# Attention inside a fused attention and feed-forward kernel: a projection in two steps over two turns, and weighted sums counted in half blocks of 256 queries

## The chip, the cores and the metric

The kernel runs on one core of a Trainium2 chip. The metric is the device time of one launch in microseconds (us). Its engines are TensorE (PE in the profile, matmuls; PEld are its weight loads), VectorE (DVE), ScalarE (ACT), GpSimd (POOL) and SyncE (SP, here a queue that issues DMAs). Each engine takes its instructions in the order of the program, and waits at each until what it needs has been made.

## The reference, cut to what matters

The input is 4 batches of 1024 tokens with 256 features.

```python
x = x + layernorm(attention(layernorm(x)))     # 16 heads of 16 features, softmax over 1024 keys
x = x + layernorm(ffn(layernorm(x)))           # silu gate, two 1024x1024 layers with gelu, 1024 -> 256

qkv    = xn @ Wqkv.T
scores = q @ k.T / 4                           # per batch and head, 1024 x 1024
attn   = exp(scores - max) / (sum + 1e-6)
y      = (attn @ v) @ Wout.T
```

The change lies in the attention alone. The kernel computes exponentials without subtracting the maximum first, folds the greatest exponential in later (the `top` tiles), and falls back to a general version if a bound says that this isn't safe.

## The kernel before, in words

**Tiles and units.** The attention is a list of 512 tiles (L514): for each of 4 batches b, 4 groups g of 4 heads, 2 halves h of 512 queries, 8 blocks c of 128 keys, and 2 pairs u of heads. Sixteen tiles make a unit (b, g, h). For one tile, `exponentials` (L520) issues two score matmuls into one of three PSUM buffers (`s`, two banks each) and one ScalarE instruction that writes `e` into a ring in SBUF that holds 8 tiles (`RING`). For two tiles of the same c, which I call a block, `weigh` (L530) multiplies the exponentials of 4 heads with the values of the block's keys: 4 matmuls over 512 queries, each of which the profile shows as two instructions (float32), so 8 instructions for a block. They add up in `acc`, one PSUM bank, over the 8 blocks of a unit. `rise` (L537) keeps the greatest exponential of each query on VectorE. At the end of a unit `unit_end` (L760) transposes `acc` out on VectorE, and `divide` adds the steps that normalise.

**Turns.** The loop at L1335 runs in turns. A turn makes 3 tiles (`TURN`, L1339; `make` keeps at most 8 tiles made and not yet weighed), then weighs blocks made in earlier turns, one or two of them: all that are there, but only one where `side.next_is_heavy()` says that a heavy step comes next (L1346). With 3 tiles to a turn, turns with one block and with two alternate. A unit's end cuts the weighing of its turn short (L1357), since `acc` has one buffer. Then the turn calls `side.take` (L1366).

**Side work.** All other attention work is cut into `Step`s (L74), which stand in chains in `Side` (L663). In each turn `take` (L697) runs at most one step that uses TensorE, and as many others as `room` allows, which is a budget of VectorE time: `ROOM` less what `rise` took, less the work of the tensor step that comes. `gap` is the least number of turns after the step before in its chain. A step built with `heavy=True` is also `patient` (L79), unless set otherwise (L754, L771): it isn't run in a turn that is `tired`, that is, one that weighed two blocks, or the one after a heavy step (L681, L712, L1362).

**The steps that the change touches.** `project` of the prologue (L378) makes q or k of one half of the queries for 8 heads of the next batch: 8 matmuls (two over the features, c, times four slots), 16 instructions in the profile as `p` at L321, into the one PSUM bank of the pool `misc` (L258). Then ScalarE copies the rounded high part (`cq..hi`, `ck..hi`, L386) and VectorE computes the low part (`lo`, L387); both read the bank. There are 8 such steps for each batch; of those for the first batch 4 run ahead of the loop. `values` (L368) makes v: 32 instructions, `pv`. `project` of `ending` (L613) is the output projection: 32 instructions, `py`. All three take their bank from `misc`, and so do the transposes (`pt`, 4 instructions), the bounds (`pn`, 2) and the flag (`pr`, 6).

**What hangs on the projections.** When all of a group's q and k are there, `stack` (L489) copies them into the operands of the scores (`sk`, `sq`) with 32 DMAs on the SP queue, 4 or 6 in a turn. `begin` (L728) builds the next batch's chain, in which the second half of the heads (`qk1`) comes with a gap of 2 turns.

After the last tile the feed-forward part runs, which the change leaves as it is.

Of the kernel before, what the change touches and what calls it, by code (L numbers as in the profile page):

```python
# [22 lines left out]
SLOT = 32  # L23
# [4 lines left out]
RING = 8  # L28
TURN = 3
# [44 lines left out]
class Step:  # L74


    def __init__(self, run, gap=0, tensor=True, heavy=False, work=0):
        self.run, self.gap, self.tensor, self.heavy, self.work = run, gap, tensor, heavy, work
        self.ready, self.patient = lambda: True, heavy  # L79


class Norms:
# [47 lines left out]
def tile_fast(ctx: ExitStack, tc: tile.TileContext, x, wqk, wv, wo, w1, w1s, w2, w2s, h1, h1s, h2, h2s, w3, w3s, out, bad):  # L130
# [65 lines left out]
    with ExitStack() as actx, ExitStack() as rctx:  # L196
# [132 lines left out]
        def prologue(b, space, copy):  # L329
# [36 lines left out]
                return run  # L366

            def values(t0):  # L368
                def run():
                    pv = space(f"pv_{b}_{t0}").rearrange("p (t d) -> p t d", d=D)  # L370
                    for i in range(2):
                        for c in range(DC):
                            by_slots(pv[:, i, :], st["xT"][:, c, (t0 + i) * P : (t0 + i + 1) * P], wv_sb[:, c, :], start=c == 0, stop=c == DC - 1)
                    copy(cv[:, t0 : t0 + 2, :], pv)

                return run

            def project(w, m, h):  # L378
                def run():
                    pp = space(f"p{w}_{b}_{m}_{h}")  # L380
                    for c in range(DC):
                        heads = wqk_sb[:, c, w, HPT * m : HPT * (m + 1), :].rearrange("p h d -> p (h d)")
                        by_slots(pp, heads, st["xT"][:, c, h * NQ : (h + 1) * NQ], start=c == 0, stop=c == DC - 1)
                    hi, lo = (cq[w, m, k][:, h * NQ : (h + 1) * NQ] for k in ("hi", "lo"))
                    scale = 1.0 if w else 1.0 / math.sqrt(DH)
                    to_scalar(hi, pp, scale)  # L386
                    nc.vector.scalar_tensor_tensor(lo, pp, scale, hi.bitcast(F32), ALU.mult, ALU.subtract)  # L387

                return run
# [63 lines left out]

            norm = [[Step(gather(h, i), 1, False, work=1.6) for i in range(0, TPQ, 2)] + [Step(root(h), 0, False, work=0.3)] for h in range(NH)]
            xt = [[Step(apply(h, i), 1, False, work=1.2) for i in range(0, TPQ, 2)] + [Step(transposes(h, c), 1 if c else 2, work=1) for c in range(DC)] for h in range(NH)]
            qk = [[[Step(project(w, m, h), 1, heavy=True, work=1) for w in (1, 0)] for h in range(NH)] for m in range(DC)]
            v = [Step(values(t), 1, heavy=b > 0, work=1) for t in range(0, NT, 2)]
            flags = []
            for m in range(DC):
                flags.append([Step(total(m), 1, False, work=1.7)])  # L460
# [66 lines left out]
                nc.tensor.matmul(s[:, a, :], stacks[1, g % 2, u][r, c * P : (c + 1) * P], stacks[0, g % 2, u][r, h * NQ : (h + 1) * NQ], start=True, stop=True)  # L527
            nc.scalar.activation(pair(k)[:, u], s, AF.Exp)  # L528

        def weigh(k, acc):  # L530

            b, g, _, c, _ = tiles[k]
            assert slotted[g % 2][:2] == (b, g) and c < slotted[g % 2][2]
            for i in range(HPG):
                nc.tensor.matmul(acc[SLOT * i : SLOT * (i + 1), :], vaug[g % 2][:, c, i, :], pair(k)[:, i // 2, i % 2, :], start=c == 0, stop=c == NT - 1)  # L535

        def rise(k):  # L537

# [61 lines left out]
        def ending(b, h, copy):  # L600

            st = {}

            def transposes(c):
                def run():
                    if c == 0:
                        st["oT"] = work.tile([P, DC, NQ], F32, tag="oT", name=f"oT_{b}_{h}", bufs=1)
                        st["y"] = (both if h else work).tile([P, TPQ, D], F32, tag="y", name=f"y_{b}_{h}", bufs=1)
                    nc.vector.transpose(st["oT"][:, c, :], on[h][:, c].rearrange("p j s -> p (j s)"))

                return run

            def project(t0):  # L613
                def run():
                    py = misc(f"py_{b}_{h}_{t0}").rearrange("p (t d) -> p t d", d=D)
                    for i in range(2):
                        for c in range(DC):
                            by_slots(py[:, i, :], st["oT"][:, c, (t0 + i) * P : (t0 + i + 1) * P], wo_sb[:, c, :], start=c == 0, stop=c == DC - 1)
                    (copy if b == B - 1 else to_scalar)(st["y"][:, t0 : t0 + 2, :], py)
# [31 lines left out]
            steps = [Step(transposes(c), 1, False, work=0.7) for c in range(DC)] + [Step(project(t), 2, heavy=True) for t in range(0, TPQ, 2)]  # L651
            tail = (
                [Step(gather(i), 1, False, work=1.6) for i in range(0, TPQ, 2)] + [Step(root, 0, False, work=0.3)]
                + [Step(apply(i), 2 if b == B - 1 and not i else 1, False, work=1.2) for i in range(0, TPQ, 2)] + [Step(residual(i), 1, False, work=1) for i in range(0, TPQ, 2)]
            )
            if b < B - 1:

                return steps + [Step(lambda: side.add(tail), 0, False)]
            opened = Step(open_ffn, 0, False)
            opened.ready = lambda: not ends[b, 0][0]  # L660
            return steps + ([opened] if h == NH - 1 else []) + tail

        class Side:  # L663


            def __init__(self):
                self.first, self.rest, self.slot = [], [], 0
                self.room = 0.0
                self.tired = False

            def add(self, steps, first=False):
                chain = [list(steps), self.slot]
# [24 lines left out]
            def take(self, room=math.inf, spare=0.0):  # L697
# [30 lines left out]
        def begin(b):  # L728

            if b + 1 < B:  # L730
# [29 lines left out]
        def unit_end(b, g, h):  # L760
# [544 lines left out]
        for h in range(NH):  # L1305
            for step in xt[h][TPQ // 2 :]:
                step.run()
            for w, step in zip((1, 0), qk[0][h]):
                if (h, w) == (0, 0):
                    compact(0)  # L1310
                step.run()
# [14 lines left out]
        made = seen = weighed = 0  # L1326

        def make(end):

# [5 lines left out]
        while weighed < len(tiles):  # L1335
            n = end = made
            end += TURN
            before, risen = weighed, seen
            make(end)  # L1339
            if made == len(tiles):  # L1340
                n = made
# [1 line left out]
                rise(k)  # L1343
                seen += 2

            if n - weighed >= 4 and made - weighed + TURN - 2 <= RING and tiles[weighed][3] != NT - 2 and side.next_is_heavy():  # L1346
                n = weighed + 2
            while weighed + 2 <= n:
                b, g, h, c, _ = tiles[weighed]
                if c == 0:  # L1350
                    accs[b, g, h] = ps_acc.tile([P, NQ], F32, tag="acc", name="acc")
                weigh(weighed, accs[b, g, h])
                weighed += 2
                if c == NT - 1:
                    unit_end(b, g, h)
# [254 lines left out]
```

## Time and profile before

| | before |
|---|---|
| median of 3 runs | 1233.38 us (1233.04 to 1235.36) |
| the profiled execution's own time | 1230.5 us |
| its span | 1228.7 us |
| mean granted TensorE clock | 0.991 |
| 30 to 190 us: busy PE, DVE, ACT | 151.15, 107.83, 134.06 us of 160 |
| 190 to 331 us | 136.01, 103.48, 124.30 us of 141 |
| 331 to 472 us | 137.77, 102.92, 125.91 us of 141 |
| 472 to 594 us | 111.14, 85.78, 112.72 us of 122 |

The loop over the turns runs from about 30 to 594 us of the span; the four stretches are roughly the four batches. What follows to 1228.7 us is the feed-forward part. A row of the profile gives the line, the engine, the operation, what is written and read, the shapes, and how many instructions there were; a row of the timeline gives start and length in us of instructions of the same kind that follow on each other. Matmuls overlap, so that a group's length is longer by its last instruction's tail than the time until the next group starts; where I give the cost of a group on PE, I take the distance from its start to the next group's start.

### The profile page before, as it was taken

What the parts mean: (1) busy time and instruction counts of PE and PEld (TensorE: products, weight loads), DVE (VectorE), ACT (ScalarE), POOL (GpSimd) and SP (SyncE); (2) the same over time, 40 slices, a digit from 0 to 9 for tenths busy, and PEclk for the clock granted to TensorE, in tenths of its full rate; (3) what the DMA queues carried; (4) which work ended last, traced back from release to release, by engine and by line L of the source; (5) the groups of instructions that cost most, each with busy time, mean ns of one, the idle gap of its engine ahead of it and who ended that gap; (6) DMA issues with size and microseconds to landing.
All of it is one profiled execution on the core that took longest, in us unless ns stands there. A gap on an engine that the chain in (4) does not pass through costs nothing.

```text
span 1228.7 us, 20496 instructions
## 1 busy us (share of the span) xinstructions
PE 1168.3 (95%) x7618; PEld 697.0 (57%) x7618; DVE 841.3 (68%) x1500; ACT 884.7 (72%) x1049; POOL 204.4 (17%) x279
## 2 busy tenths in 40 slices
PE   7999999999999999989999999999999999999993
PEld 2333333333333333323578888877888878888783
DVE  3577579865787667667685756867578676784756
ACT  4788798998889899998557565576656766566651
POOL 6212124444435342000000000000000000000000
PEclk9999999999999999999999999999999999999997
DMA  5675756766566676554314341354512545126401
GB/s 144 171 188 138 177 123 153 182 164 159 141 169 159 168 183 134 104 130 128 104 35 137 121 154 52 103 171 147 178 60 96 177 151 178 64 82 197 155 9 37
DMA packets 78669, 163.61 MB, mean 133 GB/s; under 512 B 14688, under 2 KB 40928, under 8 KB 78560
## 3 DMA queue, kind: packets, MB, share of 16 engines
q1 hardware_dynamic: 68624, 131.27, 39.2%
q0 software_dynamic: 9408, 30.42, 8.0%
q8 instruction: 62, 1.02, 0.3%
q10 hardware_dynamic: 528, 0.52, 0.1%
q14 instruction: 47, 0.39, 0.1%
HBM read 98.71 MB, written 29.88 MB: 105 GB/s over the span
## 4 chain that ended last, share of the span: by engine, by line
PE 62%; ACT 15%; DVE 12%; issue 6%; DMA 3%; SPq 1%; POOL 1%; ACTq 0%; POOLq 0%; DVEq 0%
PE ph L1012 27%; PE acc L535 10%; ACT e L528 10%; PE pg L933 9%; PE s L527 7%; PE p L321 4%; DVE lo L907 2%; PE py L321 2%; ACT hi L903 2%; DVE top L544 2%; PE pv L321 1%; PE pz L1117 1%; SPq L475 1%; DVE w L1023 1%; ACT w L1000 1%
## 5 line engine op out<-in xcount | busy, mean ns | idle before, releaser
L528 ACT ACTIVATE e<-s 128x1024 f32<-128x1024 f32 x512 | 480.8, 1041 | 36.9 <-PE s L527 24.3
L535 PE MATMUL acc<-e,vaug 128*32 128x512 f32 x2048 | 257.4, 605 | 2.9 <-POOL vaug L505 2.7
L527 PE MATMUL s<-sq,sk 64*128 64x512 f32 x1024 | 194.3, 451 | 23.9 <-ACT e L528 20.3
L527 PEld LDWEIGHTS s<-sq,sk 64*128 64x128 f32 x1024 | 87.5, 185 | 184.5 <-ACT e L528 167.8
L1012 PE MATMUL ph<-hi,sq 128*128 128x512 f32 x448 | 178.1, 398 | 0.9 <-DVE w L1023 0.9
L1012 PE MATMUL ph<-hi,sk 128*128 128x512 f32 x448 | 176.7, 394 | 0.0
L1012 PE MATMUL ph<-lo,sq 128*128 128x512 f32 x448 | 176.6, 394 | 0.0
L1012 PE MATMUL ph<-lo,sk 128*128 128x512 f32 x448 | 176.5, 394 | 0.0
L107 POOL TENSOR_TENSOR rstd<-ve,minus_half 128x4 f32<-128x4 f32 (+1 forms) x34 | 38.4, 1129 | 755.8 <-DVE ve L105 644.8
L544 DVE TENSOR_TENSOR top<-top,e 128x512 f32<-128x512 f32 x192 | 137.6, 716 | 20.3 <-ACT e L528 15.6
L535 PEld LDWEIGHTS acc<-e,vaug 128*32 128x32 f32 x2048 | 49.5, 109 | 104.8 <-issue 97.5
L907 DVE TENSOR_TENSOR lo<-c,hi 128x1024 fp32r<-128x1024 f32 x48 | 58.3, 1222 | 66.0 <-ACT hi L903 66.0
L907 DVE TENSOR_TENSOR lo<-g,hi 128x1024 fp32r<-128x1024 f32 x48 | 58.8, 1224 | 57.6 <-ACT hi L903 57.3
L1012 PEld LDWEIGHTS ph<-hi,sq 128*128 128x128 f32 x448 | 84.1, 188 | 21.6 <-DVE w L1023 2.2
L1012 PEld LDWEIGHTS ph<-hi,sk 128*128 128x128 f32 x448 | 84.1, 188 | 20.0
L1012 PEld LDWEIGHTS ph<-lo,sk 128*128 128x128 f32 x448 | 84.1, 188 | 19.9
L1012 PEld LDWEIGHTS ph<-lo,sq 128*128 128x128 f32 x448 | 84.2, 188 | 19.2
L1000 ACT ACTIVATE c<-ph,h_scale 128x512 f32<-128x512 f32 x64 | 40.5, 684 | 50.2 <-PE ph L1012 50.2
L935 ACT ACTIVATE sg<-pg,w_scale 128x512 f32<-128x512 f32 x64 | 43.6, 687 | 35.4 <-PE pg L933 33.6
L321 PE MATMUL p<-xT,wqk_sb 128*32 128x512 f32 x512 | 60.7, 593 | 5.9 <-ACT wqk_sb L209 2.6
L1117 PE MATMUL pz<-w_sb,lo 128*128 128x256 f32 x256 | 61.6, 284 | 2.9 <-DVE lo L907 2.9
L936 DVE SCALAR_TENSOR_TENSOR g<-pg,w_scale,sg 128x512 f32<-128x512 f32 x64 | 47.6, 745 | 23.7 <-ACT sg L935 23.7
(183 smaller groups left out, 1730.5 us busy)
## 6 DMA issues: line engine op xcount, KB each, us to landing
sq<-h_f SPq DMA_DIRECT2D x56, 512.0 KB, 4.2
sk<-h_f SPq DMA_DIRECT2D x56, 512.0 KB, 4.6
w<-in_h_dram POOLq DMA_DIRECT2D x32, 256.0 KB, 6.0
h_f<-wr POOLq DMA_DIRECT2D x16, 512.0 KB, 4.4
x<-in_h_dram SPq DMA_DIRECT2D x16, 512.0 KB, 3.5
top_d<-top SPq DMA_DIRECT2D x30, 256.0 KB, 2.3
folded<-top_d SPq DMA_DIRECT2D x30, 256.0 KB, 3.4
h_f<-wr POOLq DMA_DIRECT2D x16, 384.0 KB, 3.8
```

Source lines behind the costliest of these rows:

```text
L321: nc.tensor.matmul(o[j : j + SLOT, :], w[:, j : j + SLOT], i, **flags)
L527: nc.tensor.matmul(s[:, a, :], stacks[1, g % 2, u][r, c * P : (c + 1) * P], stacks[0, g % 2, u][r, h * NQ : (h + 1) * NQ], start=True, sto ...
L528: nc.scalar.activation(pair(k)[:, u], s, AF.Exp)
L535: nc.tensor.matmul(acc[SLOT * i : SLOT * (i + 1), :], vaug[g % 2][:, c, i, :], pair(k)[:, i // 2, i % 2, :], start=c == 0, stop=c == NT - 1)
L544: nc.vector.tensor_max(top, top if c > 1 else pair(k - 2)[:, :, :, 0:P], pair(k)[:, :, :, 0:P])
L907: nc.vector.tensor_sub(self.lo[i].t, self.raw[i].t, self.hi[i].t.bitcast(F32))
L933: nc.tensor.matmul(p[:, k, :], homes[n][d][:, m * P : (m + 1) * P], half[:, d, :], start=d == j == 0, stop=d == DC - 1 and j == 1)
L935: nc.scalar.activation(sg, p[:, 0, :], AF.Silu, scale=scales["w1"][:, m : m + 1])
L936: nc.vector.scalar_tensor_tensor(x[i, h][c // 2].t[:, c % 2, :], p[:, 1, :], scales["w2"][:, m : m + 1], sg, ALU.mult, ALU.mult)
L1000: nc.scalar.activation(o.t[:, j, :], (o.t if src is None else src)[:, j, :], AF.Gelu, scale=scale[:, m : m + 1])
L1012: nc.tensor.matmul(p[:, j, :], w, half, start=start and c == n == 0, stop=c == HC // 2 - 1 and n == 1, skip_group_check=True,)
L1117: nc.tensor.matmul(p[:, j, :D], half[:, (t0 + j) * P : (t0 + j + 1) * P], homes["w3"][c], start=c == order[0] and n == 0, stop=c == order[ ...
```

## The change

`project` of the prologue runs in two steps: the first issues the matmuls of c = 0 and opens the bank, the second, at the earliest in the next turn, those of c = 1 and the two copies. The new flag `split` makes `take` do this. While a bank is open (`Side.open`) no tensor step of another chain is run. These steps are no longer heavy; the heavy ones (`pv` of batches 1 to 3, `py`) all wait while a turn is tired, and a second half's output projection waits until the first half's is issued. The room that a step's work takes off is now counted in full in both turns of a split step.

The weighing is counted in half blocks (256 of the 512 queries): 3 to a turn, 2 where a heavy step comes next, 4 where 5 or more tiles are waiting. If one half block is left to do, `weigh` does the first 256 queries of a block, and the next turn the other 256; the flag that clears the bank is set on the block's first half alone.

```diff
-        def weigh(k, acc):
+        def weigh(k, acc, q0=0, q1=NQ):
...
-                nc.tensor.matmul(acc[SLOT * i : SLOT * (i + 1), :], vaug[g % 2][:, c, i, :], pair(k)[:, i // 2, i % 2, :], start=c == 0, stop=c == NT - 1)
+                nc.tensor.matmul(
+                    acc[SLOT * i : SLOT * (i + 1), q0:q1], vaug[g % 2][:, c, i, :], pair(k)[:, i // 2, i % 2, q0:q1],
+                    start=c == 0 and q0 == 0, stop=c == NT - 1, skip_group_check=True,
+                )
```

```diff
             def project(w, m, h):
-                def run():
-                    pp = space(f"p{w}_{b}_{m}_{h}")
-                    for c in range(DC):
+                def run(*parts):
+                    if 0 in parts:
+                        st["pp"] = space(f"p{w}_{b}_{m}_{h}")
+                    pp = st["pp"]
+                    for c in parts:
...
+                    if 1 not in parts:
+                        return
                     hi, lo = (cq[w, m, k][:, h * NQ : (h + 1) * NQ] for k in ("hi", "lo"))
...
-            qk = [[[Step(project(w, m, h), 1, heavy=True, work=1) for w in (1, 0)] for h in range(NH)] for m in range(DC)]
+            qk = [[[Step(project(w, m, h), 1, work=1, split=True) for w in (1, 0)] for h in range(NH)] for m in range(DC)]
```

```diff
-                if not step or slot - chain[1] < step.gap or step.tensor and not free:
+                if not step or slot - chain[1] < step.gap or step.tensor and not (free and self.open in (None, chain)):
                     return None
-                return step if step.ready() and not (step.patient and self.tired) else None
+                return step if step.ready() and not (step.heavy and self.tired) else None
...
             def next_tensor(self, slot):
 
+                if self.open:
+                    return self.open[0][0]
...
-                self.room = min(self.room, 0.5) + room - (step.work - step.heavy if step else 0)
+                self.room = min(self.room, 0.5) + room - (step.work if step and not step.heavy else 0)
...
-                        step.run()
+                        if step.split:
+                            step.run(0)
+                            chain[0].insert(0, Step(lambda run=step.run: run(1), 1, work=step.work))
+                            self.open = chain
+                        else:
+                            if step.tensor and self.open is chain:
+                                self.open = None
+                            step.run()
...
                 for step in qk1:
-                    step.gap, step.patient = 2, False
+                    step.gap = 2
...
                 last = ending(b, h, to_scalar if (b, h) == (B - 1, NH - 1) else to_vector)
-                for step in last:
-                    step.patient = False
```

```diff
+            before = (b, h - 1) if h else (b - 1, NH - 1)
+            steps[0].ready = lambda: before not in ends or not any(step.tensor for step in ends[before][0])
```

```diff
-            if n - weighed >= 4 and made - weighed + TURN - 2 <= RING and tiles[weighed][3] != NT - 2 and side.next_is_heavy():
-                n = weighed + 2
-            while weighed + 2 <= n:
+            halves = TURN if n - weighed < TURN + 2 else TURN + 1
+            if halves == TURN and made - weighed + half + TURN - 2 <= RING and tiles[weighed][3] != NT - 2 and side.next_is_heavy():
+                halves = TURN - 1
+            side.tired = side.tired or halves > TURN
+            while halves and weighed + 2 <= n:
                 b, g, h, c, _ = tiles[weighed]
-                if c == 0:
+                if c == 0 and not half:
                     accs[b, g, h] = ps_acc.tile([P, NQ], F32, tag="acc", name="acc")
-                weigh(weighed, accs[b, g, h])
+                q0 = NQ // 2 * half
+                q1 = NQ if half or halves > 1 else NQ // 2
+                weigh(weighed, accs[b, g, h], q0, q1)
+                halves -= (q1 - q0) // (NQ // 2)
+                half = int(q1 < NQ)
+                if half:
+                    break
                 weighed += 2
                 if c == NT - 1:
                     unit_end(b, g, h)
...
-                side.tired = side.tired or weighed - before >= 4
```

`values` and the output projection get the same two-part form, but their steps still run both parts at once.

More of the change, by code (lines that the diff above doesn't have):

```diff
@@ L74, with __init__ @@
 class Step:
-    def __init__(self, run, gap=0, tensor=True, heavy=False, work=0):
-        self.run, self.gap, self.tensor, self.heavy, self.work = run, gap, tensor, heavy, work
-        self.ready, self.patient = lambda: True, heavy
+    def __init__(self, run, gap=0, tensor=True, heavy=False, work=0, split=False):
+        self.run, self.gap, self.tensor, self.heavy, self.work, self.split = run, gap, tensor, heavy, work, split
+        self.ready = lambda: True
 class Norms:
@@ L368, in values, with run @@
             def values(t0):
-                def run():
-                    pv = space(f"pv_{b}_{t0}").rearrange("p (t d) -> p t d", d=D)
-                    for i in range(2):
+                def run(*parts):
+                    if 0 in parts:
+                        st["pv"] = space(f"pv_{b}_{t0}").rearrange("p (t d) -> p t d", d=D)
+                    pv = st["pv"]
+                    for i in parts:
                         for c in range(DC):
                             by_slots(pv[:, i, :], st["xT"][:, c, (t0 + i) * P : (t0 + i + 1) * P], wv_sb[:, c, :], start=c == 0, stop=c == DC - 1)
-                    copy(cv[:, t0 : t0 + 2, :], pv)
+                    if 1 in parts:
+                        copy(cv[:, t0 : t0 + 2, :], pv)
                 return run
             def project(w, m, h):
-                def run():
-                    pp = space(f"p{w}_{b}_{m}_{h}")
-                    for c in range(DC):
+                def run(*parts):
+                    if 0 in parts:
+                        st["pp"] = space(f"p{w}_{b}_{m}_{h}")
+                    pp = st["pp"]
+                    for c in parts:
                         heads = wqk_sb[:, c, w, HPT * m : HPT * (m + 1), :].rearrange("p h d -> p (h d)")
                         by_slots(pp, heads, st["xT"][:, c, h * NQ : (h + 1) * NQ], start=c == 0, stop=c == DC - 1)
+                    if 1 not in parts:
+                        return
                     hi, lo = (cq[w, m, k][:, h * NQ : (h + 1) * NQ] for k in ("hi", "lo"))
@@ L455, in prologue @@
             xt = [[Step(apply(h, i), 1, False, work=1.2) for i in range(0, TPQ, 2)] + [Step(transposes(h, c), 1 if c else 2, work=1) for c in range(DC)] for h in range(NH)]
-            qk = [[[Step(project(w, m, h), 1, heavy=True, work=1) for w in (1, 0)] for h in range(NH)] for m in range(DC)]
-            v = [Step(values(t), 1, heavy=b > 0, work=1) for t in range(0, NT, 2)]
+            qk = [[[Step(project(w, m, h), 1, work=1, split=True) for w in (1, 0)] for h in range(NH)] for m in range(DC)]
+            v = [Step(lambda run=values(t): run(0, 1), 1, heavy=b > 0, work=1) for t in range(0, NT, 2)]
             flags = []
@@ L613, in project, with run @@
             def project(t0):
-                def run():
-                    py = misc(f"py_{b}_{h}_{t0}").rearrange("p (t d) -> p t d", d=D)
-                    for i in range(2):
+                def run(*parts):
+                    if 0 in parts:
+                        st["py"] = misc(f"py_{b}_{h}_{t0}").rearrange("p (t d) -> p t d", d=D)
+                    py = st["py"]
+                    for i in parts:
                         for c in range(DC):
                             by_slots(py[:, i, :], st["oT"][:, c, (t0 + i) * P : (t0 + i + 1) * P], wo_sb[:, c, :], start=c == 0, stop=c == DC - 1)
+                    if 1 not in parts:
+                        return
                     (copy if b == B - 1 else to_scalar)(st["y"][:, t0 : t0 + 2, :], py)
@@ L649, in residual @@
                 return run
-            steps = [Step(transposes(c), 1, False, work=0.7) for c in range(DC)] + [Step(project(t), 2, heavy=True) for t in range(0, TPQ, 2)]
+            steps = [Step(transposes(c), 1, False, work=0.7) for c in range(DC)] + [Step(lambda run=project(t): run(0, 1), 2, heavy=True) for t in range(0, TPQ, 2)]
+            before = (b, h - 1) if h else (b - 1, NH - 1)
+            steps[0].ready = lambda: before not in ends or not any(step.tensor for step in ends[before][0])
             tail = (
@@ L667, in __init__ @@
                 self.first, self.rest, self.slot = [], [], 0
-                self.room = 0.0
-                self.tired = False
+                self.room, self.open, self.tired = 0.0, None, False
             def add(self, steps, first=False):
@@ L1310, in tile_fast @@
                     compact(0)
-                step.run()
+                step.run(0, 1)
                 for i, copy in enumerate(copies(0, w, h * NQ, (h + 1) * NQ)):
@@ L1325, in tile_fast @@
         side.add([s for k in blocks for s in round_weights(*k)] + [s for k in corners for s in round_corners(*k)])
-        made = seen = weighed = 0
+        made = seen = weighed = half = 0
         def make(end):
@@ L1337, in tile_fast @@
             end += TURN
-            before, risen = weighed, seen
+            risen = seen
             make(end)
```

## The prediction

> **What bounds the kernel now.** I read the busy slices first.
>
> ```profile
> PE   7999999999999999989999999999999999999993
> ACT  4788798998889899998557565576656766566651
> PEclk9999999999999999999999999999999999999997
> ```
>
> The attention is the first 19 slices of 30.7 us. In them PE is full and ACT nearly so, at an almost full granted clock. A full digit doesn't mean that PE is at its peak, so I went on to the costliest groups.
>
> ```profile
> L528 ACT ACTIVATE e<-s 128x1024 f32<-128x1024 f32 x512 | 480.8, 1041 | 36.9 <-PE s L527 24.3
> L535 PE MATMUL acc<-e,vaug 128*32 128x512 f32 x2048 | 257.4, 605 | 2.9 <-POOL vaug L505 2.7
> L321 PE MATMUL p<-xT,wqk_sb 128*32 128x512 f32 x512 | 60.7, 593 | 5.9 <-ACT wqk_sb L209 2.6
> ```
>
> ACT loses 36.9 us ahead of exponentials, 24.3 of it waiting for scores: PE has no even lead. The timeline of PE shows why. First two turns around a projection:
>
> ```profile
> 299.75 1.90 PE L321 MATMUL p<-xT,wqk_sb 128*32 128x512 f32 x16
> 301.58 0.96 PE L527 MATMUL s<-sq,sk 64*128 64x512 f32 x6
> 302.47 1.92 PE L535 MATMUL acc<-e,vaug 128*32 128x512 f32 x16
> 304.32 1.29 PE L527 MATMUL s<-sq,sk 64*128 64x512 f32 x6
> 305.54 1.06 PE L535 MATMUL acc<-e,vaug 128*32 128x512 f32 x8
> 306.42 1.90 PE L321 MATMUL p<-xT,wqk_sb 128*32 128x512 f32 x16
> ```
>
> Start to next start: p 1.83, three tiles' scores 0.89, two blocks 1.85, scores 1.22, one block 0.88. The cycle is 6.67. Its pieces with scores at 0.89 both times make 6.34; 0.33 is a wait in the second score group, and ACT's timeline names it:
>
> ```profile
> 301.71 0.60 ACT L324 ACTIVATE ck1hi<-p 128x512 fp32r<-128x512 f32 x1 [0.58 <-PE p L321]
> 302.21 5.60 ACT L528 ACTIVATE e<-s 128x1024 f32<-128x1024 f32 x6
> 308.39 0.60 ACT L324 ACTIVATE cq1hi<-p 128x512 fp32r<-128x512 f32 x1 [0.58 <-PE p L321]
> ```
>
> ACT sits 0.58 until the long p is done, then copies (0.49 until the next starts) and makes six exponentials; PE's third score of the light turn needs a PSUM buffer that ACT hasn't freed yet. Each waits for the other once in a cycle. ACT's own need is 6 x 0.905 (spacing of exponentials back to back) + 0.49 = 5.92, so PE's 6.34 is the bound that could be reached.
>
> Then turns with no side step, late in the attention:
>
> ```profile
> 508.58 1.06 PE L535 MATMUL acc<-e,vaug 128*32 128x512 f32 x8
> 509.58 0.49 PE L527 MATMUL s<-sq,sk 64*128 64x512 f32 x2
> 510.29 0.51 PE L527 MATMUL s<-sq,sk 64*128 64x512 f32 x2 [0.21 <-ACT e L528]
> 511.20 0.50 PE L527 MATMUL s<-sq,sk 64*128 64x512 f32 x2 [0.41 <-ACT e L528]
> 511.63 1.92 PE L535 MATMUL acc<-e,vaug 128*32 128x512 f32 x16
> 513.49 0.97 PE L527 MATMUL s<-sq,sk 64*128 64x512 f32 x6
> ```
>
> ```profile
> 508.29 5.61 ACT L528 ACTIVATE e<-s 128x1024 f32<-128x1024 f32 x6 [0.19 <-PE s L527]
> 514.09 5.61 ACT L528 ACTIVATE e<-s 128x1024 f32<-128x1024 f32 x6 [0.19 <-PE s L527]
> ```
>
> PE waits for ACT at scores, yet ACT runs dry once behind each two-block weighing: its six take 5.80 from start to start instead of 6 x 0.905 = 5.43. So 0.37 is lost in two turns because weighing comes in lumps of 1.85 and 0.88.
>
> Cutting the PE timeline from 30 to 594 us at each first score gives 169 turns: 25 with one block and p (mean 4.00, at best 3.60), 3 with two blocks and p, 24 with one block alone, 55 with two alone, 25 with a pv or py, 37 with something short (pt, pn, pr) or at the end.
>
> **The change part by part.**
>
> *Projections in halves.* Nothing is added or taken from the 16 instructions. Half a p is 0.86, and 0.97 where scores follow: a block is 0.88 ahead of p but 1.00 ahead of scores (508.58 to 509.58), so the passage to scores costs 0.11. A turn becomes 0.89 + three half blocks 1.31 + 0.97 = 3.17, twice that 6.34, in place of 6.67. In both turns PE is behind ACT's need (2.72 and 3.21 with the copy) by little or nothing, and no PSUM wait is left: the third score of the next turn comes some 3.8 us after the end of p, the exponential that frees its buffer about 3.3. From the turns: 25 x (4.00 - 3.60) is 10.0 us, less one wait of 1.5 us at 82 us for VectorE that has another cause. I take -8, between 0 and -8.5.
>
> *Even weighing.* Where no step disturbs it, the new count runs, by its rules: three half blocks a turn, and at unit ends one, two or four. Written out over three units (48 tiles, 16 turns): 11 turns with three, 3 with four, one with two, one with one. Two-block lumps fall from one turn in two to 3 in 16. The 24 cycles of turns with no step lose 24 x 0.37 = 8.9 us now; five eighths of that is 5.5. I take -5; the ends are 0 (heavy steps and unit ends break the rhythm everywhere) and -8.9.
>
> *Price of the split blocks.* In those 48 tiles 6 of 24 blocks are split, so about 64 of 256, each with 8 more matmuls. The nearest row has the same 32-column form over 256 columns:
>
> ```profile
> 259.06 1.91 PE L321 MATMUL pv<-wv_sb,xT 128*32 128x256 f32 x32
> 260.90 1.13 PE L527 MATMUL s<-sq,sk 64*128 64x512 f32 x6
> ```
>
> 32 instructions over 256 columns take 1.84, 16 over 512 take 1.83: by the row 512 more instructions cost about 0.3 us. The Trainium skill speaks against the change here: "TensorEngine Tiling (Array Packing)", section Instruction Overhead, gives each matmul about 60 cycles, which at the 2.4 GHz of "TensorE: Matmul & The Clock Gate" is an estimate of 25 ns and 512 x 0.025 = 12.8 us, more than the whole gain. The page itself adds that one column takes as long as 60, which makes it a floor under short matmuls, and 256 columns are far above it. I take the row, +0.3. A gain is excluded, since the same columns stream.
>
> *The open bank.* New is a wait: the first half of the next projection needs the `misc` bank, which ACT and DVE read after p's end. Behind it in PE's queue stand the next turn's scores, and ACT behind those. At 294.89 p ended and DVE's low part was done at 296.35, 1.46 later; at the earliest the next half asks 0.89 + 1.31 = 2.20 after p. Where VectorE first did a 1.21 us sum (145.11), the low part ended 2.08 after. So the cover is 0.1 to 0.7 us; `qk1` has a free turn between. At most 16 steps follow at once; at 0.5 each that is 8. I take +1, from 0 to +8.
>
> *Heavy steps.* pv keeps its pattern of one block and then two: 0. Two py that now run beside two blocks (4.7 mean) would wait: -0.3 at best, taken as 0.
>
> *VectorE's room.* Each split turn sets aside 1 unit, where a heavy p set aside none, so that norms, squares and divisions come some turns later. A turn has about 3 units less 1, the steps need about 64 in 43 turns: 1.5 a turn. It fits; I take 0, from -1 (11.2 us of ACT's waits are for `top`, which then has a freer DVE) to +3.
>
> *DMAs.* `qk1` takes three turns a step in place of two, 12 turns for 8. For batch 2 its last p ended at 308, and its copies are asked for at about 361: covered by some 50 us, and 4 more turns are 13. In the first batch it is tight: SP issues without a pause from 104 to 138, PE waits at 138.4 for `sq` (1.3 us), and the following scores make it 2.7 in all. If PE comes there 3 us earlier SP doesn't: I take +2, from 0 to +3.5. GpSimd's rounding steps are paced by turns, whose number is set by 512 tiles at 3; its queue idles at half. The feed-forward part has the same instructions: 0.
>
> Sum: -8 - 5 + 0.3 + 1 + 2 = -9.7, say -10: from the profiled execution's 1230.5 (span 1228.7 and 1.8 around it) to 1220.5. The median lies 2.9 above that execution, and I take the same difference off it: 1233.4 - 10 = 1223.4, rounded to 1223.
>
> **Rivals.**
>
> *More than that.* Beyond PE's own pieces (169 x 1.00 for scores and the passage, 256 x 0.87 for blocks, the steps at 1.73, 0.48, 0.2) the turns from 30 to 472 us hold 40 us of waits, in ACT-bound turns too. If projections spread over more turns level these as well, half of it goes: -20, 1213. For it: PE idles in turns with no step while it is late in those with p. Against: a lead of three PSUM buffers can't carry over more than one turn.
>
> *Given back.* The open bank costs its 8, SP takes its 3.5, or the count says four at every second turn (5 tiles wait there) and thereby keeps heavy steps off: -13 + 11 = about -2, 1231. For it: 2.7 us of PE's waits for the bank show already. That the rhythm of threes hardly ever runs is the same case: then -8 + 3.3 is all, 1229.
>
> *Slower.* Split blocks cost an issue price per matmul, in the turns where PE is the bound. At 25 ns it is 12.8 - 10 = +3, 1236. It decides from 10.0/512 = 20 ns on; below, the change is still faster. The pv row speaks against it.
>
> **How the numbers follow.** The sum's case 0.57 (1223); more 0.18 (1213); given back 0.18 (1229 to 1231); slower 0.07 (1236). About 0.2%, 2.5 us, is what a measurement of this kernel can tell from no change, so the line lies at 1230.9: the last 0.18 splits into 0.11 faster and 0.07 the same. Faster 0.86, same 0.07, slower 0.07. The range goes from 1213 to 1231: it leaves out the far half of "more" and the slower case.
>
> **What would show it.** Right: cycles with p at about 6.35 in the timeline; rows of `acc` with both 512 and 256 columns and some 500 more matmuls at L535; half blocks of 0.43; ACT's wait for `s` well under 24.3 us; attention's end near 584. Wrong: waits of PE at `p` for DVE `lo` or ACT `hi`; a larger wait for `sq` near 135 us; half blocks above 0.6; or most turns still with 8 and 16 `acc` instructions.

## The result and the profile after

| | before | changed |
|---|---|---|
| median (range) of 22 runs each | 1234.46 us (1230.16 to 1241.16) | 1229.49 us (1225.46 to 1232.08) |
| ratio, 95% interval | | 0.9956 (0.9944 to 0.9968) |
| the profiled execution, its span | 1230.5, 1228.7 us | 1232.08, 1230.2 us |
| first to last exponential | 565.93 us | 564.31 us |
| last exponential to the end | 637.5 us | 637.5 us |

The change makes the kernel 0.44% faster, about 5.4 us by the ratio. I had forecast 10: the direction was right, the size half of it. Batches b and groups g are counted from 0 below, as in the code.

First a trap: of the two profiled executions the changed one is the longer, by 1.5 us. The slices of the page after say where that is from.

```profile
PE   7999999999999999999999999999999999999993
PEclk8999999999999999999999999999999999999997
```

PEclk has an 8 in the first slice where before has a 9. In this execution PE ran at half clock for part of the start-up: one `p` took 3.62 us in place of 1.92, and the first exponential started at 28.42 us, not 25.30. The start-up has the same instructions in both kernels, and the first exponential of the executions below begins anywhere from 25.4 to 28.6. These 3.1 us are not the change's. So I compare what lies between the first and the last exponential, and rest no verdict on one execution.

The timeline of PE, after, where projections run (start, length, instructions):

```profile
114.68 0.96 PE L534 MATMUL s<-sq,sk 64*128 64x512 f32 x6
115.57 1.50 PE L542 MATMUL acc<-e,vaug 128*32 128x256 f32 x16
116.89 1.04 PE L321 MATMUL p<-xT,wqk_sb 128*32 128x512 f32 x8
...
121.03 0.97 PE L534 MATMUL s<-sq,sk 64*128 64x512 f32 x6
```

Scores, three half blocks, half a `p`: two turns take 121.03 - 114.68 = 6.35 us, where one cycle before took 6.67 and I forecast 6.35. The groups of the loop by shape, 30 to 594 us, show the split blocks:

```profile
L542 PE MATMUL acc<-e,vaug 128*32 128x256 f32 x752 | 59.8, 390 | 1.6 <-POOL vaug L512 1.6
```

752 instructions over 256 queries are 94 half blocks, so 47 blocks were split (376 more instructions), not 64.

The bookkeeping is done on ScalarE. Its waits in the loop, first of the kernel before (total, times, longest), those ahead of the copies of q and k:

```profile
ACT ck1hi L324 <- PE p L321: 8.1, 8, 3.1
ACT cq1hi L324 <- PE p L321: 5.9, 8, 1.4
ACT cq0hi L324 <- PE p L321: 4.7, 6, 2.1
ACT ck0hi L324 <- PE p L321: 2.7, 6, 0.8
```

and those of the changed kernel:

```profile
ACT e L535 <- PE s L534: 44.1, 53, 2.9
...
ACT e L535 <- DVE top L554: 2.9, 2, 2.7
...
ACT ck1hi L324 <- PE p L321: 0.3, 1, 0.3
```

The 21.4 us of waiting for a long `p` have gone, down to 0.9 in all, and 8.3 of the 11.2 us for `top`. But the wait for scores rose from 24.3 to 44.1. Over all exponentials and copies of the loop, those of `y` included (8.5 before, 10.1 after), ScalarE's idle time fell from 66.6 (36.7 + 21.4 + 8.5) to 64.8 us (53.8 + 0.9 + 10.1), as little as the loop got shorter. Some of the 44.1 is the old waiting under a new name. What is new is found in PE's waits, after:

```profile
PE s L534 <- DMA sq<-cq1lo: 7.4, 5, 2.9
```

Before, PE waited once for this operand, 1.3 us. Here is the second longest of the five, the start of group g = 2 of batch b = 1 on PE:

```profile
245.31 0.50 PE L534 MATMUL s<-sq,sk 64*128 64x512 f32 x2
248.60 0.47 PE L534 MATMUL s<-sq,sk 64*128 64x512 f32 x1 [2.79 <-DMA sq<-cq1lo]
```

The DMA queue of SP shows why the operand was late:

```profile
231.53 3.36 SPq L482 DMA_DIRECT2D sq<-cq1lo  x4
241.93 0.33 SPq L575 DMA_DIRECT2D folded<-top_d  x1
242.31 2.41 SPq L482 DMA_DIRECT2D sq<-cq1hi  x4
244.76 2.49 SPq L482 DMA_DIRECT2D sq<-cq1lo  x4
```

with, in SP's waits,

```profile
SPq L575 <- DVE den L562: 7.0, 1, 7.0
```

From 234.9 to 241.9 SP stands at the load of `folded`, and the last eight copies of the operand stand behind it; the last is issued at 246.7 and lands at 249.0, the group's first score was at 245.3. The same place before, SP and then the group's first scores:

```profile
237.88 0.52 SPq L565 DMA_DIRECT2D folded<-top_d  x1
238.45 3.98 SPq L475 DMA_DIRECT2D sq<-cq1hi  x4
242.47 2.49 SPq L475 DMA_DIRECT2D sq<-cq1lo  x4
...
247.39 1.34 PE L527 MATMUL s<-sq,sk 64*128 64x512 f32 x6
```

There the load went as soon as SP came to it, all copies were issued by 244.96, and PE didn't wait. It was close even so: the last copy landed at 247.7.

**The chain behind it, read in the code.** `folded` has one buffer. A unit's division (`run` in `divide`) is its last reader. For the units of a batch's first group this division stands back until the output projections of the same half of the batch before are issued (`unit[0][-1].ready` in `unit_end`). Before, output projections weren't patient; now they wait for a turn that isn't tired and for an open bank. In the traces the four `py` of batch 0 start at 188.1, 195.7, 205.1 and 213.6 us before and at 193.6, 206.1, 226.3 and 240.1 after. Counted from the first exponential, the last one comes at 188.3 before and at 211.7 after. So the division is late, the next unit's load of `folded` waits, and SP's queue is in order. This is the theory called L in the expectations; its rivals are that late `py` cost by themselves, that the split blocks cost, and that SP's queue was as heavy before the change.

### The profile page after: what moved, and what is told of

Its sections match the earlier page's. It is cut to its first block, busy times and chain, and to the rows that moved or that the text cites. A ratio compares the mean times of both kernels' runs of the same rounds, so it can differ in the third digit from the quotient of the medians.

```text
span 1230.2 us, 21266 instructions
## 1 busy us (share of the span) xinstructions
PE 1169.1 (95%) x7994; PEld 710.1 (58%) x7994; DVE 841.5 (68%) x1500; ACT 885.1 (72%) x1049; POOL 209.1 (17%) x279
## 4 chain that ended last, share of the span: by engine, by line
PE 58%; DVE 12%; ACT 12%; SPq 6%; DMA 6%; issue 5%; ACTq 0%; POOL 0%; POOLq 0%; DVEq 0%
PE ph L1034 27%; PE acc L542 9%; PE pg L955 8%; ACT e L535 6%; PE s L534 6%; SPq L482 5%; PE p L321 3%; DVE lo L929 2%; ACT hi L925 2%; PE py L321 2%; DVE top L554 1%; DMA sq<-cq1lo 1%; DMA folded<-top_d 1%; PE pz L1139 1%; DVE w L1045 1%
## 5 line engine op out<-in xcount | busy, mean ns | idle before, releaser
L535 ACT ACTIVATE e<-s 128x1024 f32<-128x1024 f32 x512 | 483.1, 1043 | 53.8 <-PE s L534 44.1
L542 PE MATMUL acc<-e,vaug 128*32 128x512 f32 (+1 forms) x2424 | 258.7, 539 | 2.9 <-POOL vaug L512 2.9
L534 PE MATMUL s<-sq,sk 64*128 64x512 f32 x1024 | 189.3, 446 | 25.3 <-ACT e L535 17.1
L554 DVE TENSOR_TENSOR top<-top,e 128x512 f32<-128x512 f32 x192 | 138.9, 723 | 24.3 <-ACT e L535 18.5
L542 PEld LDWEIGHTS acc<-e,vaug 128*32 128x32 f32 x2424 | 61.8, 109 | 120.5 <-issue 107.8
L321 PE MATMUL p<-xT,wqk_sb 128*32 128x512 f32 x512 | 69.3, 622 | 4.7 <-ACT wqk_sb L209 2.6
L957 ACT ACTIVATE sg<-pg,w_scale 128x512 f32<-128x512 f32 x64 | 43.6, 688 | 35.7 <-PE pg L955 31.9
```

The source lines that it names most:

```text
L321: nc.tensor.matmul(o[j : j + SLOT, :], w[:, j : j + SLOT], i, **flags)
L542: nc.tensor.matmul(acc[SLOT * i : SLOT * (i + 1), q0:q1], vaug[g % 2][:, c, i, :], pair(k)[:, i // 2, i % 2, q0:q1], start=c == 0 and q0 = ...
L554: nc.vector.tensor_max(top, top if c > 1 else pair(k - 2)[:, :, :, 0:P], pair(k)[:, :, :, 0:P])
L957: nc.scalar.activation(sg, p[:, 0, :], AF.Silu, scale=scales["w1"][:, m : m + 1])
```

## The experiments

Each was timed in five rounds beside the kernel before. Times in us follow from the ratio to it.

**The changed kernel again**, with no edit, to see whether those waits recur.

> The changed kernel once more, as the control on this chip. Both theories: 5 us below the kernel before (ratio 0.996). Theory L (late copies): the profile shows PE waiting again some 3 us for sq at the first scores of group 2 in the first two batches, at the same place in the program as in the first profile, and the granted clock falling just behind. Rival S (the gain itself is smaller: the rhythm of threes rarely runs, and split blocks cost): the waits for sq wander or vanish, and the time stays where it is.

Measured: 0.9948 (0.9930 to 0.9966). PE waits at the same two places, group 2 of batches 0 and 1, 2.16 and 2.65 us. They belong to the program, not to the execution.

**The split projections alone**: the changed kernel with the old count of whole blocks.

```diff
-            halves = TURN if n - weighed < TURN + 2 else TURN + 1
...
+            if n - weighed >= 4 and made - weighed + TURN - 2 <= RING and tiles[weighed][3] != NT - 2 and side.next_is_heavy():
+                n = weighed + 2
...
+                weigh(weighed, accs[b, g, h])
...
+                side.tired = side.tired or weighed - before >= 4
```

> Projections in two steps, output projections patient and ordered as in the changed kernel, but blocks weighed whole, one or two to a turn, as before. Theory L: the projection cycles lose their 0.33 (about -8 in sum), and the late copies take 5 to 8 back: 0 to -3 us against before. Rival S: the projections are where the gain is, so it shows the -5 of the whole change or more.

Measured: 1.0031 (1.0018 to 1.0045), slower by 3.8 us. I had expected a gain or nothing. Its timeline of PE:

```profile
400.62 1.25 PE L534 MATMUL s<-sq,sk 64*128 64x512 f32 x6
401.80 1.92 PE L542 MATMUL acc<-e,vaug 128*32 128x512 f32 x16
...
407.26 0.73 PE L534 MATMUL s<-sq,sk 64*128 64x512 f32 x4
```

The cycle is 407.26 - 400.62 = 6.64, no shorter than before. With whole blocks the turns are as uneven as ever: two blocks and half a `p` (0.89 + 1.74 + 0.97 = 3.60), then one and half a `p` (2.74). The first is as long as before's best turn with a `p`. That is why nothing is gained. The loss has another place, in PE's waits of this run:

```profile
PE s L534 <- DMA sq<-cq1lo: 4.0, 1, 4.0
PE s L534 <- DMA sq<-cq0lo: 2.6, 1, 2.6
```

Before had 1.3 and 0.3 us for these operands. The two waits lie in group 3 of batch 0 and group 0 of batch 3, which take 42.47 and 38.44 us in place of 39.23 and 34.59. That is 7.1 of the 8.6 us by which this execution's loop is longer (574.53 for 565.93 from the first to the last exponential). So late copies cost here too, and the run doesn't give the price of splitting alone.

**The half blocks alone**: the kernel before with the new count; a turn is tired if it really did more than three half blocks.

```diff
-            if n - weighed >= 4 and made - weighed + TURN - 2 <= RING and tiles[weighed][3] != NT - 2 and side.next_is_heavy():
-                n = weighed + 2
+            halves = TURN if n - weighed < TURN + 2 else TURN + 1
...
+                did += (q1 - q0) // (NQ // 2)
...
-                side.tired = side.tired or weighed - before >= 4
+                side.tired = side.tired or did > TURN
```

> Projections whole and heavy as before, output projections as before, but the weighing in half blocks, three to a turn (a turn counts as tired if four were really done). Theory L: output projections are on time, so no wait for sq is added in the second batch; even weighing gives its -3 to -5. Rival S: split blocks cost as much as they bring, 0 to +2 against before.

Measured: 0.9981 (0.9964 to 0.9997), -2.3 us. The parts alone give +3.8 and -2.3, sum +1.5; together they give -5.4, so the parts don't simply add.

What made the 2.3 us is not shown. This execution's loop is no shorter than before's (566.68 for 565.93), and the mean granted clock was 0.9907 over these 14 runs, 0.9882 over the 35 of the kernel before beside them. Within one kernel the time falls by about 1.1 us for each 0.001 of that clock (one slope through the runs of all kernels, each around its own mean; in these 14 runs from 1231.25 us at 0.993 to 1239.53 at 0.987), so that a clock higher by 0.0025 is worth an estimated 2.7 us. Whether even weighing raised the clock or had luck with it, no run tells. What it does in the trace is that ScalarE's wait for `top` falls from 11.2 to 2.7 us.

**Output projections as eager as before**, in the changed kernel.

```diff
-                return step if step.ready() and not (step.heavy and self.tired) else None
+                return step if step.ready() and not (step.heavy and step.patient and self.tired) else None
...
-            steps = [Step(transposes(c), 1, False, work=0.7) for c in range(DC)] + [Step(lambda run=project(t): run(0, 1), 2, heavy=True) for t in range(0, TPQ, 2)]
+            steps = [Step(transposes(c), 1, False, work=0.7) for c in range(DC)] + [Step(lambda run=project(t): run(0, 1), 2, heavy=True, patient=False) for t in range(0, TPQ, 2)]
```

> The changed kernel with one edit: output projections don't wait for turns that aren't tired (as before the change). Theory L: they come some 15 us earlier in the second batch, the folded DMA no longer holds up SP, the wait for sq at group 2 of the second batch is gone, and with it 3 to 4 us: -8 to -9 against before. Rival S: two more turns with two blocks and an output projection, +0.5 against the changed kernel, -4 to -5 against before.

Measured: 0.9919 (0.9898 to 0.9941), -10.0 us. The `py` start at 194.6 to 219.4, and group 2 of batch 1 begins without a wait: the last copy lands 0.7 us ahead of the group's first score, where in the changed kernel it landed 3.7 us behind (249.0 against 245.3). Against the change it is -4.6 us, against its repetition -3.6. This alone doesn't tell whether lateness of `py` costs through SP or by itself. The next one does.

**`folded` loaded from GpSimd's queue**, in the changed kernel; `py` stays late.

```diff
-                nc.sync.dma_start(out=folded, in_=there.rearrange("i (k s) q -> (i k) s q", s=P // SLOT))
+                nc.gpsimd.dma_start(out=folded, in_=there.rearrange("i (k s) q -> (i k) s q", s=P // SLOT))
```

> The changed kernel with the folded loads (L575) issued on GpSimd's queue in place of SP's; output projections stay as late as in the changed kernel. Theory L (SP is held up by a folded load that waits for a late output projection): the last eight copies for group 2 of the second batch are issued some 7 us earlier, PE's wait there is gone, -3 to -4 against the changed kernel (1226); the wait in the first batch stays. Rival E (what helped in the eager kernel is the output projections' place in the turns, not SP): as the changed kernel, 1229 to 1230, within 1.

Measured: 0.9899 (0.9878 to 0.9920), -12.5 us. The `py` start at 189.6, 202.1, 222.3 and 235.8. From the first exponential the last one comes at 209.1, nearly as late as in the changed kernel (211.7). Yet SP, here in its timeline, goes on:

```profile
228.19 2.48 SPq L482 DMA_DIRECT2D sq<-cq1hi  x4
230.72 3.13 SPq L482 DMA_DIRECT2D sq<-cq1lo  x4
```

and PE starts the group with no wait:

```profile
241.00 0.98 PE L534 MATMUL s<-sq,sk 64*128 64x512 f32 x6
```

So late output projections cost little once SP isn't behind them. ScalarE's idle time on the measure above is 57.6 us, 9.0 less than before, and the loop 556.87, 9.1 less.

**The remaining first loads from GpSimd's queue**: output weights and scales, which share SP with the copies in the first batch; the halves of x stay on SP.

```diff
-                return lambda: nc.sync.dma_start(out=out, in_=in_)
+                return lambda: nc.gpsimd.dma_start(out=out, in_=in_)
```

> The changed kernel with the remaining first loads (wo, x of batches 2 and 3, scales) issued on GpSimd's queue. Theory L: SP is free for the copies of the first batch, PE no longer waits at group 2 (3 us and about 1 us at the halved clock) nor at group 3 of the first batch: -4 to -6 against the changed kernel. Rival E: PE would have waited for ACT there anyhow, 0 to -1.

Measured: 0.9942 (0.9921 to 0.9963). The other wait, at group 2 of batch 0, is gone: the group takes 34.36 us in place of 38.39 and 37.51 in the two executions of the changed kernel. About 1.4 of it is given back in group 3 (37.92 for 36.5), whose operand is now the late one. Overall it is 1 to 2 us against the change, inside the intervals.

**Tired only where it is true.** The change calls a turn tired if it asks for four half blocks; where a block is open it does only three.

```diff
-            side.tired = side.tired or halves > TURN
+            did = 0
...
+                did += (q1 - q0) // (NQ // 2)
...
+                side.tired = side.tired or did > TURN
```

> The changed kernel, but a turn counts as tired only if it really weighed four half blocks (the change's count says four in every second turn of the rhythm of threes, and does three). If that flag is what keeps output projections and values late: they move forward by some 10 us, and the time falls like in the eager kernel, -3 against the changed kernel. If not: values and output projections stand beside three half blocks more often, 0 to +2.

Measured: 0.9933 (0.9913 to 0.9952), and the `py` of batch 0 are back at 188.0 to 212.4. So it is mainly this flag that makes them late. The gain over the change, 3 us, lies within the two intervals.

**The price of a split block**: the kernel before, every block weighed as two halves in a row.

```diff
-                weigh(weighed, accs[b, g, h])
+                for q0 in (0, NQ // 2):
+                    weigh(weighed, accs[b, g, h], q0, q0 + NQ // 2)
```

> The kernel before, with each block weighed as two half blocks one right after the other in the same turn: the price of splitting alone, 256 splits with 8 more matmuls each (2048). By the pv row of the first trace: +1 at most against before. At 25 ns a matmul: +51 us where PE is the bound, some +30 in all. If it is over +5, the split blocks explain part of what the change lacks (a quarter of them are split there).

Measured: 1.0034 (1.0018 to 1.0051), +4.2 us for 2048 more instructions, 2.0 ns for each (the 25 ns are the prediction's estimate). Its group of the loop, by shape:

```profile
L535 PE MATMUL acc<-e,vaug 128*32 128x256 f32 x4064 | 255.4, 384 | 3.1 <-POOL vaug L505 2.8 <-DVE o L766 0.3
```

Twice the instructions and 255.4 us busy, where before had 257.4 for half as many. At that price the change's 376 cost some 0.8 us.

**The kernel before with `folded` on GpSimd's queue**: is SP's queue a burden that was there all along?

```diff
-                nc.sync.dma_start(out=folded, in_=there.rearrange("i (k s) q -> (i k) s q", s=P // SLOT))
+                nc.gpsimd.dma_start(out=folded, in_=there.rearrange("i (k s) q -> (i k) s q", s=P // SLOT))
```

> The kernel before, with its folded loads on GpSimd's queue as in the run that helped the changed kernel by 7 us. Theory L (the change made output projections late and SP waits behind them): before the change SP is never held for long by a folded load, so the edit brings 0 to -2 here. Rival Q (folded loads on SP were a cost all along, and the change has no part in it): -5 to -7, as in the changed kernel.

Measured: 0.9979 (0.9966 to 0.9992), -2.6 us. In part, yes. It gains 2.6 where the changed kernel gains 7.0 from the same line (0.9899 against 0.9956).

**Combinations** on the changed kernel: both loads on GpSimd's queue (the edits of the fifth and sixth experiment); the same with eager `py`; and `folded` with the true flag.

> The changed kernel with the folded loads and the remaining first loads on GpSimd's queue. Theory L: no group of the first two batches waits for its copies by more than 1 us; the two gains add up, less what lies in the same place: 1219 to 1221. Rival Q: GpSimd's queue becomes late in turn (rounding, sums, norms stand in it), 1222 to 1226.

> As the run with both loads on GpSimd's queue, and output projections not held back by tired turns. Theory L: with SP free the place of the output projections matters little: within 2 us of that run. Rival E (their place in the turns is itself worth something): another -3, 1217.

> The changed kernel with folded loads on GpSimd's queue and a turn tired only if it really weighed four half blocks. Theory L: as the run with the folded loads alone, 1221 to 1223, since the lateness that the flag makes is paid on SP. Rival E: -3 again, 1219.

Measured: 0.9886 (0.9868 to 0.9904), 0.9889 (0.9871 to 0.9906) and 0.9900 (0.9882 to 0.9918). With SP free, an earlier `py` adds nothing that these intervals resolve; the profiled loops, 556.54, 554.96 and 553.78 us, leave room for up to 3. The first of them, at 1220.94 us, is the version to keep; it beats both kernels, and the three can't be told from each other or from `folded` alone.

## Why the prediction was half right

**What held.** Take SP's part out on both sides: with `folded` on GpSimd's queue, the change stands to before as 0.9899 to 0.9979, which is 0.992 +/- 0.0025 (the two half-widths added in quadrature), or -9.9 +/- 3.1 us. My sum was -9.7, its +2 for the DMAs of the first batch included, and those are still there in this comparison. So the sum was sized well, within 3 us. That is partly luck, since not all its terms were: even weighing gave at most half of its -5, and the open bank cost none of its +1.

- *Projections, -8.* A tally of turns with a `p` (a turn's time less PE's own pieces) gives 14.8 us lost in 28 turns before and 6.4 in 56 after: -8.4. What I hadn't said is that the 3.17 us turn presupposes three half blocks; with whole blocks the cycle stayed at 6.64.
- *Even weighing, -5.* Too much. Alone it gives -2.3 (-4.4 to -0.4), and perhaps nothing, given the clock. By the tally 80 turns without a step lost 32.3 us before and 57 lose 31.9 after. I had counted four half blocks in 3 turns of 16; the trace has them in nearly 50 of some 175, since units end and heavy steps come everywhere. In group 2 of batch 3, where PE has hardly any side step, 32 tiles went from 31.07 to 30.19, with 28.96 as ScalarE's least (32 x 0.905).
- *Split blocks, +0.3.* By the test some 0.8. The Trainium skill's rule, "TensorEngine Tiling (Array Packing)", Instruction Overhead, read as a price added to every matmul (25 ns, the estimate of the prediction), would have put the test with 2048 more at +51 us; it was +4.2. At 256 columns it is no added price, which fits the floor that I took it for, and my *slower* rival fell.
- *Open bank, +1.* PE's waits for VectorE behind this bank were 2.7 us before (1.5 at `p`, 1.2 at `py`) and are 2.4 after (at `py`): nothing was added.
- *VectorE's room, 0.* No run changes it alone. The waits for `top` fell with the half blocks alone, where the room is counted as before, so they don't speak for it.

**What failed** is the step *Heavy steps*: "Two py that now run beside two blocks (4.7 mean) would wait: -0.3 at best, taken as 0", and with it the sum under *DMAs*. I costed the waiting of `py` in PE's turn alone, and not what hangs on it: the division, the one buffer, the load behind it in SP's queue, the copies behind the load, the next group's scores. This load is worth 7.0 us to the changed kernel and 2.6 to the one before; the difference, 4.4 us (+/- 3.4 by the intervals), is what turns -9.9 into -5.4. At equal clock, with the slope of 1.1 us for 0.001, I estimate 4.6 and 1.9, so that 2.7 is left; the rest goes with the granted clock, which was 0.9880 in the mean of the changed kernel's runs and 0.9907 with the load moved. Theory L stands: taking the cause away (eager `py`) and cutting the link (another queue) each free the group, and the cut does so with `py` nearly as late. The rivals fell: that late `py` cost by themselves (earlier ones add nothing that can be told once SP is free), that split blocks cost (2.0 ns each), and that SP's queue was as heavy before (2.6 of 7.0).

The +2 for the first batch was right in kind, and at the wrong place: I named group 3 at 138 us, and it is group 2, at 98, whose last copy lands 3.7 us behind its first score where before it landed 0.9 ahead. Taking the load away there was worth 1 to 2.

The rival *given back* named the result's cause in half a clause ("four at every second turn ... and thereby keeps heavy steps off") with SP beside it, but as two separate costs; that the first brings about the second is what I missed. The rival *more than that* did not show: ScalarE's idle time fell by 1.8 us, and by 9.0 with SP freed. Of my signs, the cycle of 6.35 and the shapes at `acc` came true (with 376 more instructions for some 500); the attention's end, forecast near 584, was 592.7 and 588.9 in the two executions. ScalarE's wait for `s` was a bad sign: it rose to 44.1 in a kernel that got faster, because its waits for `p` and `top` were handed to it. The sum of its waits was the one to name.

**What stays open.** How the 4.4 us are spread. The second execution of the changed kernel and that with `folded` on GpSimd's queue differ by 3.5 us in the loop (560.34 and 556.87): 2.2 in group 2 of batch 1 and 1.7 in groups 2 and 3 of batch 0, the places of the late copies. The ratios say 7.0. Part of the difference goes with the clock; that the waits for copies bring the clock down is made likely by the last section, but no run tests it. Nor does an interval here resolve the exact worth of the first batch's wait.

## What to carry to other kernels

When a step is allowed to come later, follow what it releases, through buffers of one and through queues that are in order, until the chain ends or reaches the engine that bounds; its own cost is the least of it. A DMA that waits for a buffer doesn't belong in the queue that feeds the critical engine. Two parts of a change that even out the same turns have to be costed together, and idle time summed over all of an engine's waits, since one wait passes to another's name.

## What the runs showed of the hardware

Behind PE's gap of 2.79 us at 245.8 the granted clock was 0.61 for the next 4 us, and the weighing there took 2.72 us to the next start. In the second execution of the same kernel, behind a gap of 2.65 us at the same place, the clock was 1.00 and the same 16 instructions took 1.43. The two rows (time and length, busy time of each engine, then the clock, third from the end):

```profile
249.00:253.00 4.00, 3.84 (x22) 1.32 (x22) 0.70 (x2) 1.94 (x2) 0.00 (x0) 0.61 0.50 111
248.10:252.10 4.00, 3.95 (x37) 1.90 (x41) 1.38 (x2) 2.65 (x3) 0.00 (x0) 1.00 0.52 111
```

So a gap of this length can cost over 1 us more than itself, and not every time; the half clock at the start (3.1 us) comes and goes in the same way. The fourteen profiled executions of this case hold 14 stretches at half clock between 30 and 575 us, of 3.4 or 6.8 us. Twelve begin within 2 us of the end of a wait of 1.3 us or more that PE had at a group's first scores; of 17 such waits 5 are followed by none. It is waits of this kind that the change adds (PE's waits for `sq<-cq1lo` are 1.3 us before, 7.4 after) and the moved load shortens (2.3).
